# Where layer 1's loads and gathers land: the places of g's parts, five tiles ahead, and a second pair of banks for odd tiles

## The chip, the cores and the metric

The kernel runs on one core of a Trainium2 chip. The metric is device time in microseconds, from launch to end. The profile's span is a little shorter than that time; both are given below. Engines are called as in the profile: PE is TensorE (PEld its weight loads), DVE is VectorE, ACT is ScalarE, POOL is GpSimd, and SP is the queue that issues most DMAs.

## The reference, cut to what matters

A graph network of four layers works on x (2708 x 512, float32) with an adjacency matrix `adj` (2708 x 2708), mostly zeros. Each layer normalizes its input, applies a ReLU, and adds its result to x. The change lies where layer 1 ends and layer 2 begins:

```python
h = relu(layernorm(x)); x = x + edge_mean(h, adj)              # layer 0
h = relu(layernorm(x)); x = x + attention(h, adj, Wk, Wq, Wv, Wo)  # layer 1
h = relu(layernorm(x))                                         # layer 2
    h = relu(adj @ (h @ W1) + b1)
    h = relu(adj @ (h @ W3) + b3)
    x = x + tanh(h @ Wf + bf)
h = relu(layernorm(x)); x = x + ((adj != 0) @ (h @ W + b)) / deg   # layer 3
```

## The kernel before, in words

Rows are cut into NT = 22 tiles of 128 (the last has 20; NFULL = 21 is its index). Layer 0 leaves x1 (its result) in DRAM and, with it, y: each row's value projection times Wo. Layer 1's attention falls, for this data, on one neighbour per row with all the weight, whose index layer 0 wrote to `idx`; so layer 1 is x2[t] = x1[t] + y[idx[:, t]], a load, an indirect DMA (a gather of 128 rows of 2 KB), and a sum. A general form of attention stands in an `If` that these inputs skip.

Layer 2's products are made in float32r, a reduced form of float32, with each operand split in three parts, hi, lo and s, so that accuracy is kept. A product is then three matmuls: hi by hi and lo by lo go to one PSUM bank (`main`, or `agg`), s by s to another (`mixed`, or `aggs`), and `sum_banks` joins the two on ACT (L495) and DVE (L496).

- `aggregate(m, get, count)` makes row tile m of adj @ g. It walks over the pieces of the adjacency matrix, two tiles each (11 pieces). For each it asks `get(t)` for the parts of g's tiles, loads the piece (`raw`, L558), splits it (a_hi on ACT, a_lo and a_s on DVE, L576 to L578), on the first pass also counts nonzeros into `cm` (L584), and issues three matmuls per tile (L595).
- `first_product(t)` is the `get` of the first pass: it makes tile t of g = h @ W1 when it is asked for the first time, that is, in the pass for m = 0. It loads x1[t] (L608), gathers y's rows (L610), sums them on POOL (L616), stores x2[t] (L617), normalizes (`norm`: stats L503 to shift L510 on DVE and ACT, the scaled copy on ACT L513), transposes on PE (L521), splits with a ReLU (`relu_parts`: v_hi on ACT L526, v_lo and v_s on DVE L527 and L530), multiplies by W1's parts (`project3`, L547), sums the banks to `go`, and splits `go` to g's parts by `split_b` (ghi on ACT L476, glo on DVE L477, gs on DVE L478, then a scaled copy of glo on ACT L481).
- After that pass, every m has one more `project3` by W3, and in the second half of layer 2 one by Wf.

What sets the order: the code is written in a layer whose scheduler, at build time, orders the instructions of each engine's queue by their place in the program, by estimated durations, and by when buffers of a pool come free; it also puts in all waits between engines. At run time each queue runs in that fixed order. So a tile that is asked for with the same name as another shares its buffers (`bufs` of them), and its first writer waits until the last user of the buffer is done. In `first_product` x's tile `xt` and y's tile `u` have three buffers each, `v_hi`, `v_lo` and `v_s` one each, `main` and `mixed` one each, `agg` and `aggs` two each; g's parts ghi, glo and gs have one buffer for every tile t, 66 in all.

Of the kernel before, what the change touches and what calls it, by code (L numbers as in the profile page):

```python
# [8 lines left out]
FP = mybir.dt.float32  # L9
FR = mybir.dt.float32r  # L10
# [4 lines left out]
ALU = mybir.AluOpType  # L15
# [4 lines left out]
P = 128  # L20
# [12 lines left out]
def kernel(  # L33
# [36 lines left out]
    def rows(t):  # L70
        return min(P, N - t * P)
# [12 lines left out]
    x1 = [dram.tile([P, D], FP, name=f"x1_{t}") for t in range(NT)]  # L84
# [55 lines left out]
    w1r = load_w(wraw, w1_d, "wr")  # L140
    y = dram.tile([N, D], FP, name="y")
    idx = const.tile([P, NT], U32, name="idx")
# [4 lines left out]
    with tc.tile_pool(name="l0_h", bufs=1) as hp, tc.tile_pool(  # L147
        name="l0_slab", bufs=2
    ) as slabs, tc.tile_pool(name="l0_w", bufs=3) as wp, tc.tile_pool(
        name="l0_acc", bufs=2, space=PSUM  # L150
    ) as ps_acc, tc.tile_pool(name="l0_small", bufs=2, space=PSUM) as ps_small, tc.tile_pool(
        name="l0_tr", bufs=2, space=PSUM
    ) as ps_tr, tc.tile_pool(name="l0_y", bufs=1, space=PSUM) as ps_y:
        h0 = hp.tile([P, NT, D], FP, name="h0")
        for t in range(NT):
            n = rows(t)
            xt = wp.tile([P, D], FP, name="xt")
            nc.sync.dma_start(out=xt[:n], in_=x[t * P : t * P + n])
            hn = wp.tile([P, D], FP, name="hn")
# [7 lines left out]
        with tc.tile_pool(name="l0_wv", bufs=1) as wvp:  # L167
            wv = wvp.tile([P, NCD, D], FP, name="wv")
            wo = load_w(wvp, wo_d, "wo")
            for h in range(H):  # L170
                nc.sync.dma_start(
                    out=wv[:, :, h * DK : (h + 1) * DK],
                    in_=wv_d[h].rearrange("(c p) k -> p c k", p=P),
                )
            wvt = transpose_weights(wvp, ps_tr, wv, "wvt")
            for r in range(NCD):
                acc = ps_y.tile([P, D], FP, name="yacc")
# [20 lines left out]
        for m in range(NT):  # L198
            n = rows(m)
            cols = slice(m * P, m * P + n)  # L200
            at = slabs.tile([P, NT, P], FP, name="at", bufs=3)
            if TAIL:
# [5 lines left out]
                out=at[:, :NFULL, :n],  # L208
# [262 lines left out]
    cm = wts.tile([P, NT, P], BF, name="cm")  # L471
    nc.gpsimd.memset(cm, 0.0)

    def split_b(hi, lo, s, v):

        nc.scalar.activation(hi, v, AF.Copy, scale=UP)  # L476
        nc.vector.tensor_tensor(lo, v, hi.bitcast(FP), ALU.subtract)  # L477
        nc.vector.scalar_tensor_tensor(  # L478
            s, lo.bitcast(FP), SHIFT, hi.bitcast(FP), op0=ALU.mult, op1=ALU.add
        )  # L480
        nc.scalar.activation(lo, lo.bitcast(FP), AF.Copy, scale=-SHIFT)  # L481

    def split_w(raw):

        w = [wts.tile([P, NCD, D], FR, name=f"w_{part}") for part in ("hi", "lo", "s")]
        for c in range(NCD):
            split_b(*(part[:, c, :] for part in w), raw[:, c, :])
        return w
# [25 lines left out]
            dst[:n], xt[:n], AF.Identity, scale=rstd[:n], bias=shift[:n]  # L514
        )

    def relu_parts(v, n):

        pt = ps_t.tile([P, NCD, P], FP, name="pt")
        for c in range(NCD):  # L520
            nc.tensor.transpose(pt[:, c, :n], v[:n, c * P : (c + 1) * P], ident[:n, :n])  # L521
        hi, lo, s = (
            wp.tile([P, NCD, P], FR, name=f"v_{part}", bufs=1) for part in ("hi", "lo", "s")
        )
        d = (slice(None), slice(None), slice(0, n))
        nc.scalar.activation(hi[d], pt[d], AF.Relu, scale=UP)  # L526
        nc.vector.scalar_tensor_tensor(  # L527
            lo[d], pt[d], 0.0, hi[d].bitcast(FP), op0=ALU.max, op1=ALU.subtract
        )
        nc.vector.scalar_tensor_tensor(  # L530
            s[d], lo[d].bitcast(FP), SHIFT, hi[d].bitcast(FP), op0=ALU.mult, op1=ALU.add
        )
        return hi, lo, s

    def project3(parts, n, w):

        hi, lo, s = parts
        whi, wlo, ws = w
        main = ps_p.tile([P, D], FP, name="main")
        mixed = ps_p.tile([P, D], FP, name="mixed")  # L540
        for c in range(NCD):
            for acc, a, b, first, last in (
                (main, hi, whi, c == 0, False),
                (main, lo, wlo, False, c == NCD - 1),
                (mixed, s, ws, c == 0, c == NCD - 1),
            ):
                nc.tensor.matmul(acc[:n], a[:, c, :n], b[:, c, :], start=first, stop=last)  # L547
        return main, mixed

    def load_piece(m, ts):  # L550
# [45 lines left out]
        return main, mixed  # L596


    w1 = split_w(w1r)
    g1, g2, hl = {}, {}, {}  # L600
    xts = {}

    def first_product(t):
        if t in g1:
            return g1[t]
        n = rows(t)
        xt = wp.tile([P, D], FP, name="xt", bufs=3)
        nc.sync.dma_start(out=xt[:n], in_=x1[t][:n])  # L608
        yt = wp.tile([P, D], FP, name="u", bufs=3)
        nc.gpsimd.indirect_dma_start(  # L610
            out=yt[:n],
            out_offset=None,
            in_=y[:, :],
            in_offset=bass.IndirectOffsetOnAxis(ap=idx[:n, t : t + 1], axis=0),
        )
        nc.gpsimd.tensor_add(xt[:n], xt[:n], yt[:n])  # L616
        nc.sync.dma_start(out=x2[t][:n], in_=xt[:n])  # L617
        hn = yt
        norm(xt, n, hn)
        main, mixed = project3(relu_parts(hn, n), n, w1)  # L620
        go = wp.tile([P, D], FP, name="go")
        if t == NFULL:
            nc.sync.dma_start(out=go[TAIL:KT], in_=b1_d.unsqueeze(0))
        sum_banks(go, main, mixed, n)
        g1[t] = g_parts(t)
        k = krows(t)
        split_b(*(part[:k] for part in g1[t]), go[:k])
        return g1[t]

    wr = load_w(wraw, w3_d, "wr")  # L630
    for m in range(NT):
        n = rows(m)
# [150 lines left out]
```

## Time and profile before

| | |
|---|---|
| median of 3 runs | 1995.32 us (1993.75 to 1999.26) |
| profiled execution | 1996.21 us, span 1994.3 us |
| mean granted TensorE clock | 0.957 |
| busy over the span | PE 1829.1 us, DVE 1243.9, ACT 722.6, POOL 117.5 |
| layer 0 | to about 664 us |
| pass m = 0 of layer 2, with all of layer 1 | about 667 to 821 us |
| rest of layer 2 and layer 3 | about 821 us to the end |

How to read the views: in the 40 slices a digit is the busy share of a slice in tenths. A window gives the busy time of each engine between two moments. A line of waits names the waiting engine, tile and line, then what released it, with the total in us, how many times, and the longest. A group has its line, engine, operation, output <- inputs, shapes and count; then busy us and the mean duration in ns; then the idle time of the engine just before, and what ended it.

### The profile page before, as it was taken

Reading aid. Unit: us, or ns where it says so; the run is one execution under the profiler, and the core shown is the slowest. Engines: PE = TensorE matmul, PEld = TensorE weight load, DVE = VectorE, ACT = ScalarE, POOL = GpSimd, SP = SyncE. Lnnn points to the kernel's source line nnn. Section 1 sums busy time; section 2 is a strip of 40 time slices with the busy share of each in tenths; the row PEclk is TensorE's granted clock in tenths of the full one; section 3 lists DMA queues with packets and bytes.
Section 4 is the critical chain, followed back from the end, with each engine's and each line's share of the span. In section 5 each row is a group of like instructions: output and inputs, shape, how many; then the busy total and the mean of one; then the engine's idle time right before and its main releaser. Section 6 shows DMA issues by size and latency. Waiting matters only on the chain.

```text
span 1994.3 us, 22061 instructions
## 1 busy us (share of the span) xinstructions
PE 1829.1 (92%) x6520; PEld 1151.9 (58%) x6520; DVE 1243.9 (62%) x2697; ACT 722.6 (36%) x1268; POOL 117.5 (6%) x122
## 2 busy tenths in 40 slices
PE   5498898898989487999999999999999999989999
PEld 2243343343433155677777774677777767557776
DVE  5877556556241477878877779666666666543333
ACT  4853332333200255433333337444455444420000
POOL 0000000000000343000000000111111111100000
PEclk9798999998989699999999999999999999989999
DMA  8754444432320444233333335333333333456774
GB/s 258 236 174 132 135 143 132 155 122 74 87 60 21 130 139 129 74 98 92 88 87 90 86 82 169 104 93 98 91 90 99 99 91 93 115 167 187 186 184 123
DMA packets 306124, 240.15 MB, mean 120 GB/s; under 512 B 33558, under 2 KB 261030, under 8 KB 303034
## 3 DMA queue, kind: packets, MB, share of 16 engines
q1 hardware_dynamic: 304286, 233.14, 40.8%
q0 software_dynamic: 1712, 5.55, 0.9%
q8 instruction: 53, 0.87, 0.2%
q14 instruction: 73, 0.60, 0.1%
HBM read 199.87 MB, written 38.74 MB: 120 GB/s over the span
## 4 chain that ended last, share of the span: by engine, by line
PE 53%; DVE 4%; issue 1%; DMA 1%; ACT 1%; POOL 0%; ACTq 0%; DVEq 0%; POOLq 0%
PE agg L595 20%; PE agg L737 11%; PE aggs L595 10%; PE main L547 5%; PE main L114 4%; PE mixed L547 2%; DVE a_lo L577 2%; PE pt L521 1%; DMA raw<-in_adj_t_dram 1%; DMA xt<-hid 1%; DVE a_s L578 1%; PE pt L693 0%; DVE glo L477 0%; DVE gs L478 0%; DVE w_s L478 0%
## 5 line engine op out<-in xcount | busy, mean ns | idle before, releaser
L266 PE MATMUL acc<-h,at 128*128 128x512 f32 (+1 forms) x968 | 448.1, 615 | 34.8 <-DVE at L261 34.8
L595 PE MATMUL agg<-ghi,a_hi 128*128 128x512 f32 (+1 forms) x968 | 398.2, 411 | 8.8 <-ACT ghi L476 8.8
L595 PE MATMUL aggs<-gs,a_s 128*128 128x512 f32 (+1 forms) x968 | 385.0, 398 | 5.3 <-DVE gs L478 2.2
L595 PE MATMUL agg<-glo,a_lo 128*128 128x512 f32 (+1 forms) x968 | 384.6, 398 | 3.4 <-ACT glo L481 2.7
L266 PEld LDWEIGHTS acc<-h,at 128*128 128x128 f32 (+1 forms) x968 | 180.7, 192 | 277.6 <-issue 239.8
L576 ACT ACTIVATE a_hi<-raw 128x256 fp32r<-128x256 f32 (+2 forms) x484 | 192.3, 397 | 316.2 <-PE agg L595 241.6
L577 DVE TENSOR_TENSOR a_lo<-raw,a_hi 128x256 fp32r<-128x256 f32 (+2 forms) x484 | 229.0, 477 | 60.0 <-ACT a_hi L576 51.7
L595 PEld LDWEIGHTS agg<-ghi,a_hi 128*128 128x128 f32 (+1 forms) x968 | 178.3, 184 | 81.4 <-issue 33.4
L578 DVE SCALAR_TENSOR_TENSOR a_s<-a_lo,a_hi 128x256 fp32r<-128x256 f32 (+1 forms) x528 | 204.4, 391 | 32.2 <-PE agg L595 0.5
L595 PEld LDWEIGHTS aggs<-gs,a_s 128*128 128x128 f32 (+1 forms) x968 | 178.3, 184 | 59.0 <-DVE a_s L578 14.2
L595 PEld LDWEIGHTS agg<-glo,a_lo 128*128 128x128 f32 (+1 forms) x968 | 178.6, 185 | 48.9 <-ACT glo L481 8.2
L737 PE MATMUL agg<-ghi,a_hi 128*128 128x512 f32 (+1 forms) x484 | 196.5, 406 | 2.6 <-ACT ghi L718 2.4
L737 PE MATMUL agg<-glo,a_hi 128*128 128x512 f32 (+1 forms) x484 | 191.9, 397 | 3.1 <-DVE glo L719 3.1
L270 DVE SCALAR_TENSOR_TENSOR xo<-acc,deg,xt 128x512 f32<-128x512 f32 (+1 forms) x22 | 16.5, 748 | 214.9 <-PE acc L266 205.5
L734 DVE TENSOR_SCALAR a_hi<-raw 128x256 fp32r<-128x256 f32 (+2 forms) x242 | 67.9, 281 | 116.4 <-PE agg L737 100.4
L547 PE MATMUL main<-w_lo,v_lo 128*128 128x512 f32 (+1 forms) x264 | 109.3, 414 | 9.3 <-DVE v_lo L527 9.1
L547 PE MATMUL main<-w_hi,v_hi 128*128 128x512 f32 (+1 forms) x264 | 110.6, 419 | 3.3 <-ACT go L495 1.7
L737 PEld LDWEIGHTS agg<-ghi,a_hi 128*128 128x128 f32 (+1 forms) x484 | 89.9, 186 | 40.2 <-DVE a_hi L734 14.3
L584 DVE SCALAR_TENSOR_TENSOR cm<-raw,cm 128x256 bf16<-128x256 f32 (+2 forms) x242 | 93.9, 400 | 29.9 <-DMA raw<-in_adj_t_dram 29.2
L737 PEld LDWEIGHTS agg<-glo,a_hi 128*128 128x128 f32 (+1 forms) x484 | 90.1, 186 | 26.4 <-DVE glo L719 6.6
L220 ACT ACTIVATE sgn<-ar 128x2708 bf16<-128x2708 f32 (+1 forms) x22 | 54.0, 2454 | 131.2 <-DVE deg L228 115.6
L547 PE MATMUL mixed<-w_s,v_s 128*128 128x512 f32 (+1 forms) x264 | 95.2, 410 | 0.4 <-DVE go L496 0.4
(121 smaller groups left out, 1924.6 us busy)
## 6 DMA issues: line engine op xcount, KB each, us to landing
raw<-in_adj_t_dram SPq DMA_DIRECT2D x630, 128.0 KB
ar<-in_adj_dram SPq DMA_DIRECT2D x21, 1354.0 KB
at<-in_adj_t_dram SPq DMA_DIRECT2D x21, 1344.0 KB
xt<-in_x_dram SPq DMA_DIRECT2D x42, 256.0 KB
xt<-x SPq DMA_DIRECT2D x42, 256.0 KB
x<-xt SPq DMA_DIRECT2D x42, 256.0 KB
x<-xo SPq DMA_DIRECT2D x21, 256.0 KB
y<-yo SPq DMA_DIRECT2D x21, 256.0 KB
```

Of the source, the lines that this page charges most:

```text
L114: nc.tensor.matmul(acc[:n], hT[:, c, :n], w[:, c, :], start=(c == 0), stop=(c == NCD - 1))
L220: nc.scalar.activation(sgn[:n], ar[:n], AF.Copy, accum_out=rsum[:n])
L266: nc.tensor.matmul(acc[:n], at[:k, t, :n], h0[:k, t, :], start=(t == 0), stop=(t == NT - 1))
L521: nc.tensor.transpose(pt[:, c, :n], v[:n, c * P : (c + 1) * P], ident[:n, :n])
L547: nc.tensor.matmul(acc[:n], a[:, c, :n], b[:, c, :], start=first, stop=last)
L576: nc.scalar.activation(hi[d], raw, AF.Copy, scale=UP)
L577: nc.vector.tensor_tensor(lo[d], raw, hi[d].bitcast(FP), ALU.subtract)
L578: nc.vector.scalar_tensor_tensor(s[d], lo[d].bitcast(FP), SHIFT, hi[d].bitcast(FP), op0=ALU.mult, op1=ALU.add)
L584: nc.vector.scalar_tensor_tensor(c, raw[:r], 0.0, c, op0=ALU.not_equal, op1=ALU.add)
L595: nc.tensor.matmul(acc[:n], a[:k, i, :n], b[:k], start=st, stop=sp)
L734: nc.vector.tensor_scalar(mask[d], raw[:k], 0.0, None, op0=ALU.not_equal)
L737: nc.tensor.matmul(acc[:n], mask[:k, i, :n], half[:k], start=(t == 0 and j == 0), stop=(t == NT - 1 and j == 1),)
```

## The change

- A new `fetch(t)` loads x1[t] into the buffer of ghi of tile t, and gathers y's rows into the buffer of glo of tile t. Five fetches stand before everything else, ahead of the split of W1; `first_product(t)` then begins with the fetch of tile t + 5.
- `first_product` sums and normalizes in these places. The parts of v are no longer `v_hi`, `v_lo`, `v_s`: hi goes into gs's place of tile t, lo into glo's, and s into one of the three old buffers in turn. At the end g's own parts take the three places.
- For odd t the product goes to the names `agg` and `aggs` of the pool `ps_a`, for even t to `main` and `mixed` as before.
- `project3` issues its twelve matmuls in the order four hi, four lo, four s, in every product of layer 2 (before: hi, lo, s for each quarter of the inner dimension).
- In `first_product` the subtraction of `split_b` (glo = go - ghi) runs on POOL instead of DVE. Splits elsewhere keep DVE.

```diff
-    def split_b(hi, lo, s, v):
+    def split_b(hi, lo, s, v, eng=nc.vector):
         nc.scalar.activation(hi, v, AF.Copy, scale=UP)
-        nc.vector.tensor_tensor(lo, v, hi.bitcast(FP), ALU.subtract)
+        eng.tensor_tensor(lo, v, hi.bitcast(FP), ALU.subtract)
...
-    def relu_parts(v, n):
+    def left_parts():
+        return tuple(
+            wp.tile([P, NCD, P], FR, name=f"v_{part}", bufs=1) for part in ("hi", "lo", "s")
+        )
+
+    def relu_parts(v, n, get=left_parts):
...
-        hi, lo, s = (
-            wp.tile([P, NCD, P], FR, name=f"v_{part}", bufs=1) for part in ("hi", "lo", "s")
-        )
+        hi, lo, s = get()
...
-    def project3(parts, n, w):
+    def project3(parts, n, w, pool=None, names=("main", "mixed")):
...
-        main = ps_p.tile([P, D], FP, name="main")
-        mixed = ps_p.tile([P, D], FP, name="mixed")
-        for c in range(NCD):
-            for acc, a, b, first, last in (
-                (main, hi, whi, c == 0, False),
-                (main, lo, wlo, False, c == NCD - 1),
-                (mixed, s, ws, c == 0, c == NCD - 1),
-            ):
-                nc.tensor.matmul(acc[:n], a[:, c, :n], b[:, c, :], start=first, stop=last)
+        main, mixed = ((pool or ps_p).tile([P, D], FP, name=name) for name in names)
+        for acc, a, b, first, last in (
+            (main, hi, whi, True, False),
+            (main, lo, wlo, False, True),
+            (mixed, s, ws, True, True),
+        ):
+            for c in range(NCD):
+                nc.tensor.matmul(
+                    acc[:n],
+                    a[:, c, :n],
+                    b[:, c, :],
+                    start=first and c == 0,
+                    stop=last and c == NCD - 1,
+                )
...
-    w1 = split_w(w1r)
     g1, g2, hl = {}, {}, {}
-    xts = {}
+    xs, ys = {}, {}
+    AHEAD = 5
+
+    def fetch(t):
+
+        n = rows(t)
+        xs[t] = gp.tile([P, D], FP, name=f"ghi{t}")
+        nc.sync.dma_start(out=xs[t][:n], in_=x1[t][:n])
+        ys[t] = gp.tile([P, D], FP, name=f"glo{t}")
+        nc.gpsimd.indirect_dma_start(
+            out=ys[t][:n],
+            out_offset=None,
+            in_=y[:, :],
+            in_offset=bass.IndirectOffsetOnAxis(ap=idx[:n, t : t + 1], axis=0),
+        )
 
     def first_product(t):
...
-        xt = wp.tile([P, D], FP, name="xt", bufs=3)
-        nc.sync.dma_start(out=xt[:n], in_=x1[t][:n])
-        yt = wp.tile([P, D], FP, name="u", bufs=3)
-        nc.gpsimd.indirect_dma_start(
...
-        nc.gpsimd.tensor_add(xt[:n], xt[:n], yt[:n])
+        if t + AHEAD < NT:
+            fetch(t + AHEAD)
+        xt, hn = xs[t], ys[t]
+        nc.gpsimd.tensor_add(xt[:n], xt[:n], hn[:n])
         nc.sync.dma_start(out=x2[t][:n], in_=xt[:n])
-        hn = yt
         norm(xt, n, hn)
-        main, mixed = project3(relu_parts(hn, n), n, w1)
+
+        def parts():
+            return (
+                gp.tile([P, NCD, P], FR, name=f"gs{t}"),
+                gp.tile([P, NCD, P], FR, name=f"glo{t}"),
+                wp.tile([P, NCD, P], FR, name=("v_hi", "v_lo", "v_s")[t % 3], bufs=1),
+            )
+
+        banks = (ps_a, ("agg", "aggs")) if t % 2 else ()
+        main, mixed = project3(relu_parts(hn, n, parts), n, w1, *banks)
...
-        split_b(*(part[:k] for part in g1[t]), go[:k])
+        split_b(*(part[:k] for part in g1[t]), go[:k], nc.gpsimd)
         return g1[t]
 
+    for t in range(min(AHEAD, NT)):
+        fetch(t)
+    w1 = split_w(w1r)
```

More of the change, by code (lines that the diff above doesn't have):

```diff
@@ L606, in first_product @@
         n = rows(t)
-        xt = wp.tile([P, D], FP, name="xt", bufs=3)
-        nc.sync.dma_start(out=xt[:n], in_=x1[t][:n])
-        yt = wp.tile([P, D], FP, name="u", bufs=3)
[L610 to L616, printed above, removed]
+        if t + AHEAD < NT:
+            fetch(t + AHEAD)
+        xt, hn = xs[t], ys[t]
+        nc.gpsimd.tensor_add(xt[:n], xt[:n], hn[:n])
         nc.sync.dma_start(out=x2[t][:n], in_=xt[:n])
-        hn = yt
         norm(xt, n, hn)
-        main, mixed = project3(relu_parts(hn, n), n, w1)
+        def parts():
[6 more added lines that the diff above has]
+        main, mixed = project3(relu_parts(hn, n, parts), n, w1, *banks)
         go = wp.tile([P, D], FP, name="go")
```

## The prediction

> **What bounds the kernel now.** I read the 40 slices first, then the windows, the waits and the groups by form of the one stage that the change rewrites.
>
> ```profile
> PE   5498898898989487999999999999999999989999
> DVE  5877556556241477878877779666666666543333
> POOL 0000000000000343000000000111111111100000
> ```
>
> A slice is 49.9 us. In most of the second half TensorE stands at 9: those loops have little to give. The hole is in slices 14 to 16 (648 to 798 us), where PE shows 4, 8, 7. There POOL works as well: it is the first pass over m, in which `first_product` makes all 22 tiles of g. The trace has its first matmul of L547 at 688.6 us and its last near 814. The window between:
>
> ```profile
> core 0: us, PE busy (x) PEld busy (x) DVE busy (x) ACT busy (x) POOL busy (x), PEclk, DMA share, GB/s
> 688.00:814.00 126.00, 103.86 (x410) 73.36 (x408) 96.02 (x213) 69.51 (x135) 45.48 (x38) 0.93 0.39 122
> ```
>
> 126 us for 22 tiles is 5.73 us a tile, and no engine fills it: DVE is busy 96.0 us, 4.36 a tile. PE's 104 us includes drain: matmuls in a row start 0.23 us apart, so 12 of L547, 3 of L595 and four transposes (some 0.45) need 3.9 us a tile. The stage runs at the pace of waits that go round in a ring:
>
> ```profile
> ACT ghi L476 <- DVE go L496: 20.7, 14, 3.3
> DVE stats L503 <- POOL xt L616: 18.5, 10, 4.2
> POOL xt L616 <- DMA u<-y,idx: 13.4, 6, 3.4
> ACT v_hi L526 <- PE main L547: 12.1, 10, 4.3
> ...
> PE main L547 <- DVE v_lo L527: 8.3, 7, 2.1
> ```
>
> Columns are total, times and longest, in us. The second and third lines are one wait: VectorE stands still for a sum on POOL that stands still for its gather. DVE idles 126 - 96 = 30 us here, and 18.5 of it is this. The fourth is the single buffer of `v_hi`; the last is the order hi, lo, hi, lo inside one bank, where the second matmul needs `v_lo`. VectorE's own rows, with POOL's:
>
> ```profile
> L478 DVE SCALAR_TENSOR_TENSOR gs<-glo,ghi 128x512 fp32r<-128x512 f32 x21 | 15.5, 736 | 0.1
> L530 DVE SCALAR_TENSOR_TENSOR v_s<-v_lo,v_hi 128x512 fp32r<-128x512 f32 x21 | 15.3, 727 | 0.1
> ...
> L477 DVE TENSOR_TENSOR glo<-go,ghi 128x512 fp32r<-128x512 f32 x21 | 14.3, 683 | 1.2 <-ACT ghi L476 1.0
> ```
> ```profile
> L616 POOL TENSOR_TENSOR xt<-xt,u 128x512 f32<-128x512 f32 x21 | 28.7, 1374 | 38.2 <-DMA u<-y,idx 15.3 <-DVE shift L510 5.0 <-DVE cm L584 3.2
> L610 POOL DMA_INDIRECT u<-y,idx x22 | 22.2, 1008 | 31.3 <-PE pt L521 8.8 <-ACT v_hi L526 7.8 <-ACT u L513 5.5
> ```
>
> After the bar stand busy us, mean ns, and the idle before with its releasers. POOL's gathers wait 31.3 us, mostly for another tile's normalization, transposes or copy (ACT u, PE pt, ACT v_hi): the three buffers of `u` and the queue's order hold them back.
>
> [...] cm at 674.63 us lasts 1.49 us beside the POOL sum of 674.53 (usually 0.41), and the longest v_s and gs take 1.58 and 1.77 against medians of 0.68. [...] here it is 1.29 (median of the sum) against 0.69, a ratio of 1.9. [...] Here the granted clock is 0.50 in 667 to 687 us, and some matmuls after a wait take 0.63 instead of 0.39.
>
> **The change part by part.**
>
> *Fetch.* x1[t] goes straight to ghi's place and y's rows to glo's. Those 44 places are all free at the start, where before three `xt` and three `u` gated the loads. Same DMAs, same bytes (22 loads of 256 KB on SP's queue, 22 gathers of about 1.0 us on POOL). With a gather issued five tiles before its sum, a landing time of 3.8 us (median; 7.3 at most) is covered by five periods of 5 us. The 13.4 us of waiting for the gather go, and most of the 18.5 us of VectorE behind it; I leave 5. New: `ghi` of tile t may not be written until x2[t] is stored from there. The store is issued after the sum, a whole normalization and product ahead of ghi: I cost it at nothing, and up to 3 us if SP holds it behind an adjacency load.
>
> *Parts of v.* hi goes to gs's place, lo to glo's, s to three buffers in turn. The 12.1 us of v_hi and 4.3 us of v_lo (DVE) behind PE's reading go. ACT has room (69.5 of 126).
>
> *Second banks.* Odd tiles use the spare agg/aggs pair, so PE does not wait for the copy of main (1.7 us on PE, 5.5 at the weight loads). The price: the second m cannot begin until tile 21, an odd one, is summed. Before, it put about ten matmuls, 2.3 us, ahead of 818 us. Bounds 0 and +3; I take +1.
>
> *Order in `project3`.* All hi, all lo, all s. Four hi matmuls are 0.92 us of cover, over a v_lo of 0.68. That removes v_lo's 8.3 us of PE idle in this stage (not added to the sum; VectorE sets it). In the 43 later products, PE idle put to v_lo is only 0.8 us from 830 to 1275 and none after; at the weight loads v_lo and v_s add up to 14.6, most of it under running matmuls. Bounds 0 and -10; I take -2.
>
> *glo's subtraction to POOL.* VectorE loses 21 instructions at 0.61 us from start to start, -12.8 us. POOL gets 22 at 1.29, so 22.2 + 30.5 + 28.4 = 81 us of 126, or 3.7 a tile: room, if nothing in its queue blocks. Two costs. VectorE's stretch by the lock is now 21 x (0.727 - 0.682) + 21 x (0.736 - 0.684) + 8 x (0.598 - 0.410) = 3.5 us for 30.5 us of POOL reading; twice the reading gives +3.5, and at most half a POOL instruction each time, 22 x 0.64 = +14. I take +6. And gs, queued on VectorE behind glo, now waits for POOL: 0.6 us more if the order is planned well, plus what POOL is late, plus everything queued on VectorE behind gs. Bounds 0 and 22 x 1.3 = 28; I take 0.4 a tile, 9 us.
>
> *Start.* Fetches come ahead of w1's split and the adjacency pieces. From 667 to 687 us DMA moves 218 GB/s already; first stats run at 683.4 although the first sum is done at 675.8, because cm and a_lo of early pieces stand before it on VectorE and wait for `raw`. At 0.25 MB each, two more loads and two more gathers ahead of `raw` are 1 MB, some 4 us at that rate. Or the stats come sooner. Bounds -4 and +6; I take 0.
>
> Sum for the stage, on VectorE's account: 96.0 - 12.8 = 83.2 busy, +6 lock, idle 30 - 13.5 - 4.3 = 12.2, +9 for gs: 110.4, or 5.0 a tile, against 126: -15.6. With +1 and -2 the total is -16.6. The profiled execution took 1996.2 us (span 1994.3 and 1.9 around it), so 1979.6; the median of the runs is 0.9 below it: **1979 us**.
>
> **Rivals.**
>
> *A. POOL's lateness eats it.* With gs's wait at 20 us (0.9 a tile) and the lock at 8, the account is 83.2 + 8 + 12.2 + 20 = 123.4, -2.6; with +1 and -2 it is -3.6, so 1992. For: POOL sums already hold VectorE for 18.5 us. Against: nearly all of that was the gather's lateness, which goes.
>
> *B. POOL becomes the bound; slower.* Its queue runs in order: a gather (1.0 to 1.3), a sum and a subtraction (each 1.29, or 1.79 as its longest now), 0.3 between them, is 3.9 to 5.8 us a tile. If the subtraction for tile t also stands waiting for ghi, with the sum of a later tile behind it, for whose stats VectorE waits, the ring closes again, one engine further on. It turns to a loss where POOL's period passes 5.73. With the stretched 4.9 and 1.3 us of waiting for ghi each tile it is 6.2: +0.5 x 22 = +11, 2006. Against: POOL's unstretched 3.7 leaves 2 us.
>
> *C. The full gain.* VectorE's idle falls to what ACT and PE force (some 5 us) and gs waits 0.1: 83 + 4 + 5 + 2 = 94, close to PE's 86. -32 and a quicker start: about 1962.
>
> *D. It does not fetch ahead in fact.* Gathers stay late in POOL's queue behind sums and subtractions, whose order is fixed before the run. Then the 13.5 us stay and only parts, banks and order work: 83.2 + 6 + 25.7 + 9 = 123.9, -2.1, and 1992 again.
>
> **How the numbers follow.** About 6 us (0.3%) is what a measurement of this kernel can tell from no change: faster is below 1989. The forecast's own case (1970 to 1988) has 0.57, C 0.13, D 0.08 and A 0.11 (of each 0.02 faster by over 6 us, and of A 0.01 slower), B 0.11 (slower). Faster 0.57 + 0.13 + 0.04 = 0.74, same 0.14, slower 0.12. The range drops B and the far half of C: 1961 to 1997.
>
> **What would show it.** Right: stats' wait for POOL under 6 us and the sum's wait for the gather near zero in this stage; x1 loads and gathers bunched before 720 us; v_hi without a wait for PE; the stage from first to last product 105 to 115 us; v_s and gs longer on average (0.75 to 0.95 us); the first product still near 688. Wrong: gs waiting over 20 us for POOL's glo (A), POOL over 85% busy with VectorE behind it (B), the first product after 694 us (the start's upper bound), or a difference in the span that arises after 830 us, where I expect only 2.

## The result, and the profile after

| | before | after |
|---|---|---|
| median of 3 runs | 1995.32 us | 2012.35 us (2009.86 to 2012.95) |
| ratio, 95% interval | | 1.0078 (1.0052 to 1.0105) |
| profiled execution (span) | 1996.21 us (1994.3) | 2012.95 us (2011.2) |

The change makes the kernel 17 us slower (0.8%). The forecast was 1979 us, and its range ended at 1997. The 40 slices of the kernel after:

```profile
PE   5498898898999278899999999899999999989999
DVE  5877556556241488778878779666666566543333
POOL 0000000000000662100000000111111111100000
```

The hole in PE's row is still there and has become deeper at its start: slices 14 to 17 read 2, 7, 8, 8 (before: 4, 8, 7, 9). POOL's 6, 6, 2, 1 stand earlier and higher than the 3, 4, 3 of before: its work has moved to the front of the stage. The stage between its first and its last matmul of L549, widened by a microsecond on either side:

```profile
core 0: us, PE busy (x) PEld busy (x) DVE busy (x) ACT busy (x) POOL busy (x), PEclk, DMA share, GB/s
703.00:828.00 125.00, 101.91 (x412) 70.98 (x412) 101.84 (x197) 72.72 (x140) 51.89 (x41) 0.93 0.20 66
```

It lasts 125 us, against 126 before. VectorE has 16 instructions less in it (197 for 213) and is busy 101.8 us where it was busy 96.0. The waits of the same stretch:

```profile
POOL glo L477 <- ACT ghi L476: 69.8, 19, 6.4
...
DVE gs L478 <- POOL glo L477: 13.9, 11, 2.2
```

Neither the sum's wait for its gather nor VectorE's wait (stats, L503) for the sum is in this list any more. The first part of v, now in gs's place, waits for no product any longer, only for the transposes that it is made from (4.1 us). What the forecast said would go has gone. VectorE's groups, by form, from 664 to 838 us:

```profile
L478 DVE SCALAR_TENSOR_TENSOR gs<-glo,ghi 128x512 fp32r<-128x512 f32 x21 | 17.6, 837 | 14.0 <-POOL glo L477 13.9
L585 DVE TENSOR_TENSOR a_lo<-raw,a_hi 128x256 fp32r<-128x256 f32 x15 | 13.9, 936 | 1.2 <-PE agg L603 1.2
...
L533 DVE SCALAR_TENSOR_TENSOR v_s<-glo,gs 128x512 fp32r<-128x512 f32 x7 | 8.3, 1182 | 0.1
```

After the first bar stand busy us and the mean in ns. A subtraction of 128x256 (a_lo) takes 0.41 us where POOL does no arithmetic (none_on_pool, below); here its mean is 0.94. The s part of v takes 0.68 there, and 1.18 here in the seven tiles that use the buffer v_s (0.96 and 0.90 in the other two buffers). All three forms read two operands from SBUF. Those of 512 columns that read one, or have the other in PSUM, have the same mean in both kernels: stats (L503) 0.67 here and 0.68 there, the lo part of v (L530) 0.68 in both, go (L496) 0.68 to 0.69 in both.

To compare kernels I use moments counted from layer 0's last store of `y`, which stands between 661.7 and 668.7 us in these executions (664.3 before, 667.2 after) in no order that follows the edits; that 2.9 us is not the change's. The table reads one profiled execution of each kernel; some lie off their median, order_only's by -4 us, sub_on_dve's by +3 and dummy_sub's by +7. **Stretch** is the sum, over VectorE's instructions with two SBUF operands from 664 to 840 us, of duration less the duration without interference (0.68 us for 512 columns, 0.41 for 256, and 0.24 to 0.29 for the few smaller ones). Tiles of g are counted from 1 here, at their split on ACT; pace is the mean distance of tiles 7 to 21. All in us:

| kernel | first product | first to last product | tiles 1 to 7 | pace | stretch |
|---|---|---|---|---|---|
| before | 24.3 | 125.2 | 33.7 | 5.75 | 6.0 |
| after | 36.6 | 123.3 | 45.4 | 4.95 | 29.3 |
| fetch_only | 36.7 | 114.8 | 39.9 | 4.72 | 20.4 |
| no_fetch | 23.8 | 126.7 | 33.5 | 5.80 | 14.2 |
| sub_on_dve | 36.8 | 108.4 | 37.2 | 4.42 | 19.0 |
| sub_only | 23.9 | 134.4 | 38.3 | 6.09 | 14.6 |
| none_on_pool | 20.6 | 128.0 | 30.9 | 5.26 | 0.0 |
| order_only | 24.3 | 123.8 | 32.3 | 5.81 | 5.7 |
| dve_old_order | 34.4 | 110.7 | 39.4 | 4.49 | 21.5 |
| dummy_sub | 36.7 | 129.3 | 44.9 | 5.24 | 42.5 |
| late_dummy | 24.2 | 131.9 | 35.9 | 6.06 | 13.5 |
| first_sums_dve | 21.0 | 118.1 | 41.6 | 4.50 | 17.2 |
| gated_sums | 32.5 | 110.7 | 32.7 | 4.77 | 12.5 |
| gated_first_dve | 20.1 | 122.2 | 34.3 | 5.44 | 14.6 |
| gated_ahead1 | 26.7 | 113.8 | 37.2 | 4.65 | 12.9 |
| after_gated | 29.5 | 125.2 | 41.4 | 5.28 | 21.4 |

So the span's +16.9 us divides up: +2.9 in layer 0; +12.3 until the first product; -3.2 from there to tile 1's split and +11.7 over tiles 1 to 7; -11.2 over tiles 7 to 21, and +0.6 to the end of the pass; then -3.4 in the rest of layer 2's first half, +6.9 in its second (from the load of `bf` to the first mask of layer 3) and +0.4 in layer 3. The steady tiles did speed up, to 4.95 us each where 5.0 was forecast. The loss is at the start and in the early tiles, with a smaller one in the second half of layer 2.

### The profile page after: what moved, and what is told of

It is laid out like the page before. It is cut to its first block, busy times and chain, and to the rows that moved or that the text cites. A ratio compares the mean times of both kernels' runs of the same rounds, so it can differ in the third digit from the quotient of the medians.

```text
span 2011.2 us, 21970 instructions
## 1 busy us (share of the span) xinstructions
PE 1827.4 (91%) x6520; PEld 1152.6 (57%) x6520; DVE 1246.2 (62%) x2675; ACT 723.0 (36%) x1268; POOL 146.8 (7%) x144
## 4 chain that ended last, share of the span: by engine, by line
PE 52%; DVE 7%; POOL 3%; issue 2%; DMA 1%; ACT 1%; ACTq 0%; DVEq 0%; POOLq 0%; SPq 0%
PE agg L603 19%; PE agg L763 11%; PE aggs L603 10%; PE main L549 4%; PE main L114 4%; PE mixed L549 2%; DVE a_lo L585 2%; PE pt L526 1%; POOL glo L617 1%; POOL glo L477 1%; DVE gs L478 1%; DVE a_s L586 1%; POOL ghi L631 1%; DMA xt<-hid 1%; DMA raw<-in_adj_t_dram 1%
## 5 line engine op out<-in xcount | busy, mean ns | idle before, releaser
L266 PE MATMUL acc<-h,at 128*128 128x512 f32 (+1 forms) x968 | 448.2, 615 | 36.7 <-DVE at L261 36.7
L603 PE MATMUL aggs<-gs,a_s 128*128 128x512 f32 (+1 forms) x968 | 386.0, 400 | 16.8 <-DVE gs L478 12.3
L585 DVE TENSOR_TENSOR a_lo<-raw,a_hi 128x256 fp32r<-128x256 f32 (+2 forms) x484 | 217.0, 452 | 73.3 <-ACT a_hi L584 68.2
L586 DVE SCALAR_TENSOR_TENSOR a_s<-a_lo,a_hi 128x256 fp32r<-128x256 f32 (+1 forms) x528 | 224.5, 432 | 27.2 <-PE aggs L603 3.8
L603 PEld LDWEIGHTS agg<-ghi,a_hi 128*128 128x128 f32 (+1 forms) x968 | 178.1, 184 | 81.8 <-issue 32.5
L592 DVE SCALAR_TENSOR_TENSOR cm<-raw,cm 128x256 bf16<-128x256 f32 (+2 forms) x242 | 99.5, 419 | 28.3 <-DMA raw<-in_adj_t_dram 17.6
L220 ACT ACTIVATE sgn<-ar 128x2708 bf16<-128x2708 f32 (+1 forms) x22 | 54.0, 2454 | 131.9 <-DVE deg L228 115.7
L709 POOL TENSOR_TENSOR u<-u,cm 128x512 f32<-128x512 f32 (+1 forms) x22 | 29.7, 1350 | 858.9 <-DVE u L496 839.2
L97 ACT ACTIVATE std<-mv,eps 128x1 f32<-128x1 f32 (+1 forms) x44 | 12.0, 286 | 197.3 <-DVE mv L95 177.4
L114 PE MATMUL yacc<-wvo,hT 128*128 128x512 f32 (+1 forms) x176 | 82.0, 610 | 0.4 <-ACT hT L109 0.4
## 6 DMA issues: line engine op xcount, KB each, us to landing
raw<-in_adj_t_dram SPq DMA_DIRECT2D x630, 128.0 KB
```

The costliest lines, as they stand in the source:

```text
L114: nc.tensor.matmul(acc[:n], hT[:, c, :n], w[:, c, :], start=(c == 0), stop=(c == NCD - 1))
L220: nc.scalar.activation(sgn[:n], ar[:n], AF.Copy, accum_out=rsum[:n])
L266: nc.tensor.matmul(acc[:n], at[:k, t, :n], h0[:k, t, :], start=(t == 0), stop=(t == NT - 1))
L585: nc.vector.tensor_tensor(lo[d], raw, hi[d].bitcast(FP), ALU.subtract)
L586: nc.vector.scalar_tensor_tensor(s[d], lo[d].bitcast(FP), SHIFT, hi[d].bitcast(FP), op0=ALU.mult, op1=ALU.add)
L592: nc.vector.scalar_tensor_tensor(c, raw[:r], 0.0, c, op0=ALU.not_equal, op1=ALU.add)
```

## The experiments

Ratios are to the kernel before in the same series of runs, with 95% intervals. The parts of the change come first, then the two places of the loss.

### Parts of the change, alone and left out

**fetch_only** is the kernel before with the fetch alone: the places, and five tiles ahead.

```diff
+    def fetch(t):  # x1[t] to ghi's place, y's rows to glo's
...
-        xt = wp.tile([P, D], FP, name="xt", bufs=3)
-        nc.sync.dma_start(out=xt[:n], in_=x1[t][:n])
...
+        xt, yt = xs[t], ys[t]
```

> The kernel before with the fetch alone: loads and gathers into the places of ghi and glo, five tiles ahead; parts, banks, order of project3 and the subtraction on VectorE stay as before. Theory S (the start: loads and gathers run far ahead, so the adjacency pieces land late, and POOL's sums stop VectorE's instructions with two SBUF inputs): first product 10 to 14 us later than before, at 698 to 703 us on the clock of before; total +4 to +12 us, since later tiles gain something from the fetch. Rival C (the new wait of gs for POOL's subtraction is the loss): no loss here, 0 to -15 us against before.

Measured: 1996.0 us against 1995.2, 1.0000 (0.9989 to 1.0011). The fetch brings the faster pace (4.72) and the late first product (+12.4) together, and they cancel; the +4 to +12 us expected did not come. The whole late start of after belongs to it.

**no_fetch** is after with the loads and gathers as they were, three buffers each.

```diff
-        xt, hn = xs[t], ys[t]
+        xt = wp.tile([P, D], FP, name="xt", bufs=3)
+        nc.sync.dma_start(out=xt[:n], in_=x1[t][:n])
+        yt = wp.tile([P, D], FP, name="u", bufs=3)
...
```

> The changed kernel with loads and gathers as before (three buffers of xt and u, issued inside first_product), the split of W1 first as before; parts, banks, order and the subtraction on POOL stay changed. Theory S: the first product is back near 688 us on the clock of before, and the total falls by 10 to 14 us to about 2000. Rival C: gs still waits 15 us or more for POOL, and the total stays above 2005.

Measured: 1999.71 us, 1.0022 (1.0013 to 1.0031). The first product is at 23.8 us again and the pace at 5.80, as before: without the fetch the other parts together bring nothing and cost 4 us.

**sub_on_dve** is after with the subtraction back on VectorE.

```diff
-        split_b(*(part[:k] for part in g1[t]), go[:k], nc.gpsimd)
+        split_b(*(part[:k] for part in g1[t]), go[:k])
```

> The changed kernel with the subtraction glo = go - ghi back on VectorE. Theory L (POOL's reading instructions stop VectorE: 29 us of stretch in the changed kernel against 6 before): stretch falls to about 15 us, the wait of gs for POOL (15 us) goes, VectorE gets 13 us of work back; the stage after the first product gets 10 us shorter, total about 2002. Theory S: the first product stays as late as in the changed kernel (12 us after that of before). Rival C: the whole 17 us go, total 1995 or less.

Measured: 1992.17 us, 0.9983 (0.9974 to 0.9991). One line is worth some 19 us (1.0078 against 0.9983), more than the whole loss. Its stage, from its first product to its last:

```profile
core 0: us, PE busy (x) PEld busy (x) DVE busy (x) ACT busy (x) POOL busy (x), PEclk, DMA share, GB/s
703.00:812.00 109.00, 95.65 (x409) 70.74 (x410) 102.72 (x216) 69.25 (x138) 23.75 (x20) 0.95 0.23 74
```

VectorE executes 19 instructions more here than in after and is busy for only 0.9 us more: what the subtraction took away from VectorE's queue, the other instructions lost to it. VectorE stands idle for 6.3 us of the window here, and for 23.2 in after's. The stage is 15 us shorter.

**sub_only** is the reverse: before, with only the subtraction of `first_product` moved to POOL.

```diff
-        split_b(*(part[:k] for part in g1[t]), go[:k])
+        split_b(*(part[:k] for part in g1[t]), go[:k], nc.gpsimd)
```

> The kernel before with only the subtraction of first_product on POOL. Theory L (POOL's reading beside VectorE's two-operand instructions costs more than the 13 us of VectorE's work that it saves): 3 to 10 us slower than before, gs waiting 12 us or more for POOL, stretch on VectorE 10 us or more instead of 6. Rival (the subtraction only hurts together with the run-ahead of gathers and sums): within 2 us of before.

Measured: 2007.43 us, 1.0048 (1.0032 to 1.0064). The move loses 10 us with no fetch beside it. Its waits from 664 to 840 us:

```profile
POOL glo L477 <- ACT ghi L476: 31.7, 15, 6.1
DVE gs L478 <- POOL glo L477: 20.8, 18, 1.7
...
DVE stats L503 <- POOL xt L616: 12.1, 9, 4.4
```

gs waits in 18 of the tiles, VectorE's other work stretches by 8.6 us, 21 subtractions at 0.61 us are saved, and the wait of stats falls from 18.5 to 12.1 us: 20.8 + 8.6 - 12.8 - 6.4 is +10 on VectorE's account. From first to last product it is +9.2.

**none_on_pool** leaves POOL no arithmetic in the stage: subtraction and sum both on VectorE.

```diff
-        nc.gpsimd.tensor_add(xt[:n], xt[:n], hn[:n])
+        nc.vector.tensor_add(xt[:n], xt[:n], hn[:n])
```

> The changed kernel with the subtraction and also the sum x1 + y on VectorE, so that POOL issues gathers only and reads no SBUF operand in this stage. Theory L: v_s, gs, a_lo, a_s and cm all at their medians of before (0.68 and 0.41 us), stretch under 2 us, no a_lo of several us; VectorE gets 26 us of work more than in the changed kernel and loses 29 us of stretch; if the lock is also what delays the start, the first product comes within 5 us of before; if it is the late adjacency pieces, it stays 8 us or more late. Total 1992 to 2002.

Measured: 1994.47 us, 0.9993 (0.9982 to 1.0004). Two of VectorE's groups, 664 to 840 us:

```profile
L478 DVE SCALAR_TENSOR_TENSOR gs<-glo,ghi 128x512 fp32r<-128x512 f32 x21 | 14.3, 682 | 0.0
L585 DVE TENSOR_TENSOR a_lo<-raw,a_hi 128x256 fp32r<-128x256 f32 x25 | 10.2, 411 | 2.3 <-PE agg L603 1.8 <-ACT a_hi L584 0.5
```

The same forms that took 0.84 and 0.94 us take 0.68 and 0.41, and the stretch is 0.0, though POOL still issues its 22 gathers (0.98 us each): the whole stretch comes from POOL's arithmetic. But the 22 sums, 0.68 us each on VectorE (1.28 on POOL in sub_on_dve), take back most of what the stretch had cost: from 664 to 812 us VectorE is busy 118.6 us here and 122.9 in sub_on_dve, and the total is that of before. The first product came at 20.6 us instead of 36.6, which I had not looked for: a sum on VectorE takes a place of its own in that queue, and stats moved with it to a place ahead of adjacency pieces (the first at 12.8 us after layer 0's last store, 27.0 in after).

**order_only** puts the new order of `project3` on the kernel before; **dve_old_order** is sub_on_dve with the old order.

```diff
-        for c in range(NCD):
-            for acc, a, b, first, last in (
+        for acc, a, b, first, last in (
...
+            for c in range(NCD):
```

> The kernel before with only the order of project3 changed (four hi, four lo, four s). Theory O (the new order costs, as the stretch from the end of layer 2's first half to the start of layer 3 is 7 to 8 us longer in all three kernels that had it, and the first half about 3 us shorter): 3 to 7 us slower than before, the second half of layer 2 530 us instead of 523, the first pass unchanged within 3 us. Rival (it is other parts' new order of the queues): as before within 2 us, second half 523.

> The changed kernel with the subtraction on VectorE and the old order in project3; fetch, places for the parts and second banks stay. Theory O: 1992 less 3 to 7, so 1985 to 1989; first product still 36 us after layer 0's last store, second half of layer 2 523 us. Rival: 1992 as with the new order.

Measured: order_only 1996.59 us against 1996.79, 1.0001 (0.9992 to 1.0011); dve_old_order 1995.95, 0.9996 (0.9985 to 1.0006). Neither moved as the theory of a costly order wanted. Still, the parts of it are visible: in all kernels with the new order the second half of layer 2 takes 527 to 531 us, in all with the old one 523 to 525; and the rest of the first half, after its first pass, is some 2.5 us shorter on average. In order_only that and a first pass shorter by 2.3 us cancel the second half's loss. order_only's waits in that second half (1208 to 1736 us):

```profile
PEld agg L600 <- DVE a_lo L582: 6.9, 20, 0.8
...
PE aggs L600 <- DVE a_s L583: 4.3, 21, 0.4
```

Before, the same two stand at 0.8 and 1.2 us. A build-time change of the queues' order would do this; that is argued, and no run takes it apart.

### Why the subtraction on POOL is dear

Two mechanisms were left: VectorE's instructions with two SBUF operands stretch beside POOL's arithmetic (the prediction's lock; 29.3 us in after, 0.0 in none_on_pool), or gs and the rest of VectorE's queue wait for POOL's result. **dummy_sub** keeps sub_on_dve's subtraction on VectorE and repeats it on POOL, into a spare buffer that nobody reads.

```diff
         split_b(*(part[:k] for part in g1[t]), go[:k])
+        copy = wp.tile([P, D], FP, name="xt", bufs=3)
+        nc.gpsimd.tensor_tensor(copy[:k], go[:k], g1[t][0][:k].bitcast(FP), ALU.subtract)
```

> The changed kernel with the subtraction on VectorE (new order kept), and besides, after each, the same subtraction once more on POOL into a spare buffer that nothing reads: POOL's work and its SBUF reading are those of the changed kernel, but gs does not wait for it. Theory L (POOL's reading stops VectorE): 1992 plus 8 to 15, so 2000 to 2007, with v_s, gs, a_lo, a_s and cm stretched as in the changed kernel. Rival C (the chain ghi, POOL, gs is what costs): within 4 us of 1992.

Measured: 2012.79 us against 1996.79, 1.0079 (1.0058 to 1.0099). That is a loss as large as after's, and beyond the 2000 to 2007 expected, though gs waits for nothing on POOL; the stretch is 42.5 us. It shows that the lock can cost this much, not what it costs in after, for two things differ: VectorE keeps its own subtraction, and both subtractions are released by the same ghi (in the first tile they start at 712.49 and 712.64 us); VectorE's took 1.49 us on average instead of 0.68. From POOL's timeline and from VectorE's in this run (start, duration, engine, line, instruction; xN is N in a row):

```profile
732.43 1.31 POOL L652 TENSOR_TENSOR xt<-go,ghi 128x512 f32<-128x512 f32 x1
733.68 6.13 POOL L631 TENSOR_TENSOR ghi<-ghi,glo 128x512 f32<-128x512 f32 x5
739.78 1.25 POOL L652 TENSOR_TENSOR xt<-go,ghi 128x512 f32<-128x512 f32 x1
```
```profile
732.15 9.43 DVE L533 SCALAR_TENSOR_TENSOR v_lo<-glo,gs 128x512 fp32r<-128x512 f32 x1
```

An s part of v (in the buffer v_lo), 0.68 us alone, stood for 9.43, through seven POOL instructions in a row; it ended 0.55 us after the seventh. In the kernel after the same is seen once, with five sums in a row on POOL and one a_lo of 0.41 us:

```profile
730.79 6.15 POOL L631 TENSOR_TENSOR ghi<-ghi,glo 128x512 f32<-128x512 f32 x5
```
```profile
730.49 6.73 DVE L585 TENSOR_TENSOR a_lo<-raw,a_hi 128x256 fp32r<-128x256 f32 x1
```

**late_dummy** avoids the collision: it is before, with one more POOL subtraction per tile at the end of the split, when VectorE has made gs; it writes `go`, which is dead by then.

```diff
         split_b(*(part[:k] for part in g1[t]), go[:k])
+        hi_, lo_, s_ = g1[t]
+        nc.gpsimd.tensor_tensor(go[:k], s_[:k].bitcast(FP), hi_[:k].bitcast(FP), ALU.subtract)
```

> The kernel before, and after each split in first_product one more subtraction on POOL (gs - ghi) into the buffer of go, which is dead by then and read by nobody: POOL reads SBUF as much as in the kernel with only the subtraction on POOL (2007), but VectorE keeps its own work, gs waits for nothing new, and POOL's instruction is not released at the same moment as a VectorE one on the same operands. If the lock alone makes the subtraction's 10.6 us: stretch on VectorE rises from 6 to about 14 us, 2003 to 2008 beside a before of 1997. If it is the wait of gs for POOL (21 us there): stretch may rise, but the total stays within 4 us of before.

Measured: 2004.61 us against 1994.84, 1.0042 (1.0025 to 1.0059). Nothing waits for the new instruction, none is saved, and it costs 10 us, as sub_only did. Its waits, 664 to 840 us:

```profile
POOL xt L616 <- DMA u<-y,idx: 22.4, 14, 3.2
DVE stats L503 <- POOL xt L616: 21.5, 11, 4.3
...
POOL go L629 <- DVE gs L478: 12.0, 4, 3.8
```

So gs' wait is not needed for a loss of this size. Two things are left in this run: 7.5 us more stretch than before, and POOL's in-order queue, which now stands for VectorE's gs (12.0 us) with gathers and sums behind it, so that over the same stretch the sum's wait for its gather grew from 17.2 to 22.4 us, and that of stats for the sum from 18.5 to 21.5. How the 10 us divide between them stays open; taking one away without the other was not tried.

### The late start and the early tiles

In after, seven loads of x1 go out on SP's queue from 669.8 us on, and the first adjacency piece `raw` behind them at 676.9. Before, two loads stood ahead of it. The other five follow from the code: five fetches stand at the top, and the first piece asks for two tiles before it is loaded, each of which fetches one more. With them the load of W3 (`wr`, 1 MB) has come ahead of the first piece, and SP waits 3.3 us until VectorE's split of W1 has read that buffer before it issues it. From SP's timelines, first before, then after:

```profile
668.14 0.43 SPq L558 DMA_DIRECT2D raw<-in_adj_t_dram  x1
669.44 1.41 SPq L558 DMA_DIRECT2D raw<-in_adj_t_dram  x3
673.15 0.37 SPq L120 DMA_DIRECT2D wr<-in_L_gnn_W_dram  x1
```
```profile
669.82 2.73 SPq L615 DMA_DIRECT2D ghi<-x  x6
675.92 0.38 SPq L120 DMA_DIRECT2D wr<-in_L_gnn_W_dram  x1
676.37 0.49 SPq L615 DMA_DIRECT2D ghi<-x  x1
676.91 0.43 SPq L566 DMA_DIRECT2D raw<-in_adj_t_dram  x1
```

Counted from layer 0's last store, the first piece is issued at 9.7 us instead of 3.8, behind 2.25 MB more of loads, and the first a_hi on ACT starts at 19.8 us instead of 8.2. VectorE's timeline in after (start, duration, line; in brackets the idle time before and its releaser):

```profile
687.04 0.43 DVE L592 SCALAR_TENSOR_TENSOR cm<-raw,cm 128x256 bf16<-128x256 f32 x1 [9.90 <-POOL ghi L631]
687.43 1.97 DVE L585 TENSOR_TENSOR a_lo<-raw,a_hi 128x256 fp32r<-128x256 f32 x1
689.43 0.42 DVE L586 SCALAR_TENSOR_TENSOR a_s<-a_lo,a_hi 128x256 fp32r<-128x256 f32 x1
690.14 1.66 DVE L592 SCALAR_TENSOR_TENSOR cm<-raw,cm 128x256 bf16<-128x256 f32 x1 [0.29 <-DMA raw<-in_adj_t_dram]
...
694.15 0.68 DVE L503 BATCH_NORM_STATS2 stats<-ghi 128x6 f32<-128x512 f32 x1
```

The first sum on POOL is done at 681.9, but stats of the first tile stand behind cm, a_lo and a_s of the first pieces. The first of them waits 9.9 us. The releaser named, POOL's sum, is not what cm reads: ACT's a_hi of the same piece starts at 686.98 after 9.2 us of waiting for `raw`, so the piece's landing is the true one. Then a_lo takes 1.97 and cm 1.66 us, beside POOL's sums of 687.83 and 690.24 us. The sums start between 680.6 and 739.9 us, the last one 15 us ahead of the seventh tile's split: the fetch was to be five tiles ahead, but nothing holds the sums, which write in place and wait for nobody. Of the stretch of 29.3 us, 8.3 lie before tile 1's split, 13.9 in tiles 1 to 7 and 7.1 in the fourteen others (before: 2.2, 1.5 and 2.2 in the like stretches).

**first_sums_dve** puts the first four sums on VectorE, on dve_old_order.

```diff
-        nc.gpsimd.tensor_add(xt[:n], xt[:n], hn[:n])
+        (nc.vector if t < 4 else nc.gpsimd).tensor_add(xt[:n], xt[:n], hn[:n])
```

> As the kernel with the subtraction on VectorE and the old order, but the sums x1 + y of tiles 0 to 3 also on VectorE, the later ones on POOL. Theory S2 (the late start comes from statistics standing in VectorE's queue behind adjacency pieces that land late, and from POOL's sums holding VectorE there): the first product moves from 36 to 21-26 us after layer 0's last store, as when all sums are on VectorE, and the total is 8 to 14 us under the same kernel without this, about 1976. Rival (the start's delay is the flood of loads itself, whatever the engine): first product at 30 or more, total within 4 us.

Measured: 1986.61 us against 1996.79, 0.9954 (0.9939 to 0.9969). The first product comes at 21.0, with the pace kept at 4.50: the first version clearly faster than before, 9 us ahead of dve_old_order. The adjacency pieces come no sooner here (the first is issued at 13.8 us): what moved is the place of stats ahead of them.

**gated_sums** leaves all sums on POOL, but writes them to three buffers, so that a sum can't run more than three tiles ahead of the normalization (also on dve_old_order).

```diff
-        xt, hn = xs[t], ys[t]
-        nc.gpsimd.tensor_add(xt[:n], xt[:n], hn[:n])
+        xt, hn = wp.tile([P, D], FP, name="xt", bufs=3), ys[t]
+        nc.gpsimd.tensor_add(xt[:n], xs[t][:n], hn[:n])
```

> The changed kernel with the subtraction on VectorE and the old order of project3, and the sum x1 + y written to the three buffers of xt instead of ghi's place, so that a sum on POOL cannot run more than three tiles ahead; loads and gathers still run ahead. Theory R (the changed kernel loses by POOL's gathers and sums running back to back, far ahead, in the first 75 us after layer 0, where they hold VectorE's two-operand instructions): tiles 1 to 7 of g take 30 to 34 us instead of 37, stretch on VectorE under 13 us instead of 21, total 4 to 8 us below the same kernel without the gate (1996 beside a before of 1997). The first product stays late, 30 us or more after layer 0's last store. Rival (the depth of the run-ahead does not matter, only how many POOL instructions read): stretch 17 us or more, total within 3 us of 1996.

Measured: 1987.83 us against 1996.8, 0.9951 (0.9933 to 0.9969). Its slices:

```profile
PE   5498898898989289999999998999999999989999
...
POOL 0000000000000352000000000111111111100000
```

The hole is two digits, 2 and 8, with 9 on both sides. The stretch fell from 21.5 to 12.5 us and tiles 1 to 7 from 39.4 to 32.7: the sums that ran ahead had slowed the early tiles.

**gated_first_dve** has both of these edits, and **after_gated** the gate on after as it is, with its subtraction on POOL.

> The same gate, and the sums of tiles 0 to 3 on VectorE. Theory R: the early start of the kernel with its first sums on VectorE (first product 21 us after layer 0's last store) and the gate's quicker first tiles add up: 1978 to 1984, below that kernel's 1987 beside a before of 1997. Rival: no better than 1987.

> The changed kernel whole, subtraction on POOL, new order, with only the sums gated by the three buffers of xt. Theory R: the block of five sums in a row that held one a_lo for 6.7 us is gone; 2012 less 8 to 14, so 1998 to 2004, and what is left over the gated kernel with the subtraction on VectorE (6 us or more) is the subtraction's own. Rival C (only the subtraction on POOL costs, by its place in the chain): 2008 or more.

Measured: 1988.33 us, 0.9952 (0.9935 to 0.9969), and 2006.42, 1.0046 (1.0031 to 1.0062). The two gains don't add: the first product comes at 20.1 us, but the pace is 5.44, and why is open. In after the gate recovers 6 us, between the two forecasts; the subtraction's cost stays.

**gated_ahead1** is gated_sums with one tile fetched ahead instead of five.

```diff
-    AHEAD = 5
+    AHEAD = 1
```

> The gated kernel (1988) with AHEAD = 1 instead of 5: the first adjacency piece stands on SP's queue behind three loads of x1 instead of seven. If the late adjacency pieces make the late start: it lands about 4 loads of 0.25 MB earlier, 3 to 5 us at 260 to 306 GB/s, and first statistics and first product come 3 to 6 us sooner (26 to 29 us after layer 0's last store instead of 32.5); total 1982 to 1986. If POOL's sums and their place in the queue make it: first product within 1 us of 32.5, total as before, 1986 to 1990.

Measured: 1986.58 us against 1994.84, 0.9948 (0.9931 to 0.9965). In gated_sums the first a_hi on ACT starts 21.3 us after layer 0's last store, behind a wait of 10.7 us. Here it starts at 8.4 us, since the first piece now goes out at 4.1 us, and the waits that are left, from 664 to 720 us, are for the next pieces:

```profile
ACT a_hi L578 <- DMA raw<-in_adj_t_dram: 9.0, 2, 7.7
```

The first product comes at 26.7 instead of 32.5 us: some 6 us of the late start come from what stands ahead of the adjacency pieces on SP's queue. The run moved two things there, four loads of x1 and the load of W3, which again follows the first piece; they were not taken apart. But tiles 1 to 7 take 37.2 instead of 32.7, and the total is the same within the intervals.

The versions clearly faster than before are these last: the fetch, the parts' places and banks, the subtraction on VectorE, the old order and either a gate or four sums on VectorE, at 0.995 of the time before. A gate with the new order and the subtraction on VectorE was not tried.

## Why the prediction was wrong, point by point

Of the 33 us between forecast and result, about 14 arose in the stage, 12 in its start, 5 behind the pass and 3 in layer 0, which the change does not touch. Two steps failed: the price of glo's subtraction on POOL, with the lock, and the price of the start.

- **Fetch.** Right in what it removes: the 13.4 us behind the gather went, and so did all 18.5 us behind the sum (5 were left in the forecast). The step's unstated assumption failed, that the sums would spread over the stage at the tiles' pace. Since they no longer wait for buffers, they run one after another behind the gathers (POOL stood idle for 0.4 us in all ahead of 21 of them), the last from 739.9 us on, and VectorE stretches where it makes the first tiles (13.9 us in tiles 1 to 7). The step set no lock against this; fetch_only has a stretch of 20.4 us for 6.0 before. No wait of ghi for the store of x2 is in after's list.
- **Parts of v.** Right: v's parts wait for no product's reading.
- **Second banks.** +1 forecast; from the last product to the end of the pass 7.2 us after, 7.4 before. Nothing, which is inside the bounds.
- **Order in `project3`.** -2 forecast. Alone it is 1.0001 in total; within after, the rest of layer 2 is 3.5 us slower net (-3.4, +6.9). "What would show it" had named a difference after 830 us as a sign of error. The bounds, 0 and -10, left no room for a loss: the step had counted the waits that the new order removes and none that it may add, such as the 6.9 and 4.3 us for a_lo and a_s in order_only.
- **glo's subtraction to POOL.** This is the step that failed in the stage. It priced the move at +2.2 us: -12.8 for VectorE's work, +6 for the lock, +9 for gs' wait. Between sub_on_dve and after, VectorE's busy time fell by 0.9 us only (102.7 to 101.8) and its idle time grew by 16.9 (6.3 to 23.2): +16. Both terms were too small. gs' wait was 15.1 us over the whole pass, inside its bounds and below rival A's mark of 20. The **lock** took back 10.3 of the 12.8 us that were saved: the stretch is 29.3 us with the subtraction on POOL and 19.0 without. Those 19.0 are themselves 13 more than before, and they belong to the fetch, for which no lock was priced. From first to last product alone the stretch is 3.4 us before, 11.0 in sub_on_dve and 20.9 after, so that the +6, with bounds +3.5 and +14, stands against +17.5: 7.6 from the fetch and 9.9 with the subtraction. Two faults: the upper bound let each POOL instruction cost half of its own time once, where one a_lo lasted 6.73 us beside a row of five sums that took 6.15; and it doubled the reading of before at the density of before, where the fetch had crowded the sums into 60 us.
- **Start.** 0 forecast, bounds -4 and +6; +12.3 measured: the second step that failed. It counted two more loads and two more gathers ahead of `raw`, 1 MB, and priced them at 4 us. Five more loads stood there and W3's 1 MB, 2.25 MB without the gathers; at the 218 GB/s that the step used, that is some 10 us (an estimate), and the first a_hi did start 11.6 us later. About 6 us went away with four of the loads and with W3's place (gated_ahead1's 26.7 against gated_sums' 32.5), and from 2 (34.4 to 32.5, on dve_old_order) to 7 (36.6 to 29.5, on after) from POOL's early sums. Both reach the product because stats stand behind the pieces in VectorE's queue: where they did not, the first product came 12 to 13 us sooner (21.0 for 34.4, 20.1 for 32.5). The prediction had read that place in the queue and then priced the bytes alone. Its mark, a first product after 694 us, was passed (703.8).
- **The sum for the stage.** 110.4 us forecast, 5.0 a tile; 123.3 measured. Part of it agrees by luck. Without the subtraction the same account gives 96.0 + 12.2 = 108.2 us, and sub_on_dve took 108.4, but with 102.7 us busy and 6.3 idle: the lock that was left out and the waits that went beyond the forecast cancel. In after the idle time, 23.2 us for 21.2, is near for a like reason. Over tiles 7 to 21 the pace is 4.95, as forecast, with the waits gone that were to go; the other 13 us are the early tiles, 7.6 us each (45.4 over six) with 13.9 us of stretch among them. Likewise gs's mean of 0.84 us lies between the 0.75 and 0.95 foretold, and that of the three v_s, (8.3 + 6.7 + 6.3) over 21, is 1.01.

Of the rivals none is the case. A had a loss through gs' wait and the lock together, 20 and 8 us; it was 15.1 and 17.5 in the stage. B is slower as it foretold, yet POOL was busy 51.9 of 125 us (85% was its mark), and in the stage VectorE waits for POOL nowhere but at gs. In late_dummy something like B's ring is seen: stats behind a sum, behind POOL's wait for gs. C's 94 us, 4.3 a tile, were nearly reached in steady tiles once the subtraction was on VectorE (4.42), but not its quicker start. D fell: the last gather was issued at 729.6 us, against 789.3 before.

## What to carry to other kernels

When a fetch is moved ahead, ask what each consumer waited for besides data: with the buffer wait gone, the consumer runs early too. Here POOL's sums ran ahead into the early tiles, where VectorE stretched by 13.9 us; a small ring of output buffers was a cheap gate (0.9951 with it, 0.9996 without). Work moved from VectorE to GpSimd need not be saved: here moving 12.8 us of subtractions made the kernel 10 us slower alone, and some 19 beside the fetch. And at the start of a stage, look at what stands ahead of its first instruction in the in-order queue, not only at bytes ahead of its load: in after the first sum was done at 681.9 us, and its stats ran at 694.15, behind the first pieces.

## What the runs showed of the hardware

The prediction had bounded VectorE's stretch at half a POOL instruction each time, 0.64 us. The runs show more. Where four or more sums on POOL followed each other without a gap, one VectorE instruction stood through four to seven POOL instructions, in each of the six kernels that have such a row: 6.73 us in after for an a_lo of 0.41, 6.59 in fetch_only, 6.17 in sub_on_dve, 7.01 in dve_old_order, 5.95 in first_sums_dve, and 9.43 in dummy_sub. It does not hold for every row: in after_gated, beside a subtraction and two sums in a row from 746.27 us on, a cm took 1.34 us and the gs after it 1.75. What decides between the two cases is open. Where a gather stood between POOL's sums, as in after's start, single VectorE instructions took 1.4 to 2.1 us.
